# Graph layer over half of a symmetric matrix: rows of tiles taken two at a time, their mirrored products summed in one half bank

## The chip, the cores and the metric

The kernel runs on one core of a Trainium2 chip. The time is device microseconds of one execution, lower is better. A core has engines that run beside one another, each with its own queue taken in order: TensorE (PE in the profile, PEld for its weight loads), VectorE (DVE), ScalarE (ACT), GpSimd (POOL), and SyncE (SP), which here only issues transfers. SBUF is the working memory of 128 partitions; [...] DRAM is the outer memory.

## The reference

Four graph layers act in turn on x (4096 nodes, 64 features) with one symmetric, sparse 4096 x 4096 matrix adj, each followed by a residual and a layernorm: a Chebyshev layer, an attention layer with two gated units, a layer of decayed ranks, and a hyperbolic layer. The change lies in the last one, and this is what it computes:

```python
def _L3_gnn_ref(x, adj, weight, bias):
    ...
    deg = jnp.maximum(adj.sum(axis=1, keepdims=True), 1e-08)
    w = adj / deg
    log_ij = _logmap(x[:, None, :], x[None, :, :], c)
    agg = jnp.einsum('ij,ijc->ic', w, log_ij)
    transformed = agg @ weight + bias
    origin = jnp.zeros_like(transformed)
    return _expmap(origin, transformed, c)
...
x = _layernorm(x + _L3_gnn_ref(x, adj, L3_gnn_weight, L3_gnn_bias), axis=-1)
```

For every pair of nodes i, j a scalar factor f of x_i and x_j multiplies adj_ij, and the weighted rows are summed over j. Both f and adj are symmetric in i and j up to factors of one node alone, so a tile of the product serves its own rows and, turned, the mirrored ones.

## The kernel before

The 4096 nodes are eight groups of 512 (GW), each of four blocks of 128. A tile (i, j) pairs row group i with column group j, 512 x 512. `seq` is the order in which the layer before finishes the groups, and "place" is a group's index in it; below, groups are called by their place. Only tiles with the column's place not below the row's are taken: 36, row by row: (0,0), (0,1) ... (0,7), (1,1), (1,2) and so on to (7,7). Eight are diagonal, 28 are not. An off-diagonal tile is loaded twice from DRAM, once as it is (`load_own`, L1301) and once mirrored (`load_mirrored`, L1307), 1 MB each, three buffers for each kind.

The loop runs over half tiles: turn n works on half n % 2 of tile n // 2. Of a diagonal tile's second half only the right 256 columns are computed (`columns`). The steps of one half:

- `product` (L1327, PE) puts a 128 x 1024 pair of products into PSUM as v, from `rights[i]`, a pair of factors of the row (rv, ro) that `right` builds once for each row, with two matmuls and two ACT copies (L1283 to L1287). Two buffers of each are in turn.
- `square` (L1336, ACT), `less_one` (L1353, DVE), `opposite` (L1345, PE), Ln (L1520) and Exp (L1521) on ACT, rt = max(v) + rt (L1545, DVE), Exp (L1547) and Ln (L1556) on ACT, the factor f (L1530, DVE), then own = own * f (L1533, DVE), two turns later.
- `turn` transposes f on PE (L1371; L1364 for a diagonal tile) into a "post" bank of two, and DVE multiplies the mirrored tile by it (L1373, 128 x 512, four for each off-diagonal tile; L1366 for a diagonal one).
- `gather` multiplies by nat_c on PE. A row i has one PSUM bank, `sums[i]`, from a pool of two. The own product (L1387) gathers in the upper 64 partitions, over the whole row of tiles. The mirrored product of the tile before (L1392) goes to the lower 64 partitions of the same bank, starts anew with each tile, and is at the end of the tile copied (row 0, L1401) or added (L1403) by DVE to `tb`, 64 x 512, at the columns of j.
- When a row ends, ACT copies the upper half to `tb` (L1406), and `finals` puts six steps (one empty, `first` to `fifth`) into the list `seam`; one step is taken at the end of a turn. They bring the group through small matmuls, the exponential map, the layernorm (L241 to L261) and to the output. The first entries of `seam` are the last groups of the layer before (L1077 to L1120).

The Python order is not the machine order: the framework schedules each engine's queue itself, except where `in_order` fixes it; dependencies through tiles and buffers become semaphores. POOL clears the buffers of `right` (L1265) and a part of tb (L1295) at the start of the layer.

Of the kernel before, what the change touches and what calls it, by code (L numbers as in the profile page):

```python
# [9 lines left out]
F32 = mybir.dt.float32  # L10
BF16 = mybir.dt.bfloat16
# [3 lines left out]
ALU = mybir.AluOpType  # L15
# [45 lines left out]
def gnn4_kernel(  # L61
# [21 lines left out]
    nc = tc.nc  # L83
    P = 128
    N, F = x.shape
    NB = N // P
    GB = 4
    GW = GB * P
    NG = NB // GB
    CB = 4  # L90
# [56 lines left out]
    with tc.tile_pool(name="tri", bufs=1) as tri_p:  # L147
# [6 lines left out]
        lower, upper = slice(0, HP), slice(HP, P)  # L154
# [301 lines left out]
    with tc.tile_pool(name="acc", bufs=1) as acc_p, tc.tile_pool(name="win", bufs=1) as win_p, tc.tile_pool(  # L456
        name="cols0", bufs=4
    ) as cols_p, tc.tile_pool(name="diag0", bufs=2) as diag_p, tc.tile_pool(
        name="ps_t0", bufs=3, space=PSUM
    ) as ps_t, tc.tile_pool(name="ps_a0", bufs=1, space=PSUM) as ps_a, tc.tile_pool(  # L460
        name="ps_p0", bufs=2, space=PSUM
# [112 lines left out]
        for g in range(NG):  # L574
# [3 lines left out]
            for c in reversed(range(NCH)):  # L578
# [40 lines left out]
                n = g * NCH + c  # L619
# [71 lines left out]
        due, n = [], 0  # L691
# [358 lines left out]
    for signed in (True, False):  # L1050
        with tc.If(any_negative > 0) if signed else cmp.Else() as block:
            cmp = block
            with tc.tile_pool(name="cols1", bufs=4 if not signed else 2) as cols_p, tc.tile_pool(name="sign1", bufs=1 if signed else 5) as sg, tc.tile_pool(
                name="tail1", bufs=1
            ) as tl, tc.tile_pool(name="ps_a1", bufs=1 if signed else 2, space=PSUM) as ps_a, tc.tile_pool(
                name="ps_p1", bufs=2, space=PSUM
# [80 lines left out]
    with tc.tile_pool(name="mask2", bufs=3) as mk_p, tc.tile_pool(name="wt2", bufs=3) as wt_p, tc.tile_pool(  # L1137
        name="ps_c2", bufs=1, space=PSUM
# [104 lines left out]
    with tc.tile_pool(name="o3", bufs=1) as op, tc.tile_pool(name="cols3", bufs=3) as cols_p, tc.tile_pool(  # L1243
# [15 lines left out]
        wh_x = op.tile([P, F], F32, name="wh_x")  # L1259
        kappa = op.tile([P, 2, NB], F32, name="kappa")  # L1260

        rvs = [op.tile([P, GW], F32, name=f"rv{q}") for q in range(2)]
        ros = [op.tile([P, GW], BF16, name=f"ro{q}") for q in range(2)]
        for t in rvs + ros:
            nc.gpsimd.memset(t, 0.0)  # L1265

# [11 lines left out]
        nc.vector.tensor_copy(spread[:, F : F + 1], pair[:, F - 1 : F])  # L1278

        def right(i):  # L1280
            q = seq.index(i) % 2
            ps = ps_p.tile([P, GW], F32, name="post", tag="post")
            nc.tensor.matmul(ps[0 : F + 2, :], lhsT=to_right, rhs=tr_a[:, gcols(i)], start=True, stop=True)  # L1283
            nc.scalar.copy(rvs[q][0 : F + 2, :], ps[0 : F + 2, :])
            ps = ps_p.tile([P, GW], F32, name="post", tag="post")
            nc.tensor.matmul(ps[0:2, :], lhsT=to_other, rhs=tr_o[:, gcols(i)], start=True, stop=True)
            nc.scalar.copy(ros[q][0:2, :], ps[0:2, :])  # L1287
            return rvs[q], ros[q]


        seq = turns_of[0] + turns_of[1]
        tiles = [(i, j) for n, i in enumerate(seq) for j in seq[n:]]
        NT = len(tiles)
        own, mirrored = {}, {}
        nc.gpsimd.memset(tb[F:P, gcols(seq[0])], 0.0)  # L1295
# [20 lines left out]
        NU = 2 * NT  # L1316
# [59 lines left out]
        def gather(t, h, tm):  # L1376

            if t is not None:
                i, j = tiles[t]
                if i == j and h == 0:  # L1380
                    sums[i] = ps_a.tile([P, GW], F32, name="sums_ps")
                bank = sums[i]
            else:
                bank = sums[seq[-1]]
            for k in (HB * h, HB * h + 1):
                if t is not None:
                    in_order(nc.tensor.matmul(  # L1387
                        bank[0:F, :], lhsT=nat_c[:, j * CB + k, :], rhs=own[t][:, k, :],
                        start=(i == j and k == 0), stop=(j == seq[-1] and k == CB - 1), skip_group_check=True,
                    ))  # L1390
                if tm is not None:
                    in_order(nc.tensor.matmul(  # L1392
                        bank[F:P, :], lhsT=nat_c[:, tiles[tm][0] * GB + k, :], rhs=mirrored[tm][:, k, :],
                        start=(k == 0), stop=(k == CB - 1), skip_group_check=True,
                    ))
            work = []
            if tm is not None and h:
                i, j = tiles[tm]
                to = tb[F:P, gcols(j)]
                if i == seq[0]:  # L1400
                    work.append(lambda: nc.vector.tensor_copy(to, bank[F:P, :]))  # L1401
                else:
                    work.append(lambda: nc.vector.tensor_tensor(to, bank[F:P, :], to, ALU.add))  # L1403
            if t is not None and h and tiles[t][1] == seq[-1]:
                g = tiles[t][0]
                work.append(lambda: nc.scalar.copy(tb[0:F, gcols(g)], bank[0:F, :]))  # L1406
                seam.extend(finals(g))
            return work
# [99 lines left out]
        while n < NU + 2 or turns or gathers:  # L1508
            if n % 2:
                load_own((n + 1) // 2)  # L1510
                load_mirrored((n - 1) // 2)
            after = gather(*gathers.pop(n)) if n in gathers else []
            turned = [w for what in turns.pop(n, []) for w in turn(what)]
            if n < NU:
                if n % 2 == 0:
                    fs[n // 2] = fp.tile([P, CB, GW], F32, name="f3")
                w, cs = ws[n][:, :, columns(n)], columns(n)
                rts[n] = el.tile([P, HB, GW], F32, name="rt3")
                rt = rts[n][:, :, cs]
                nc.scalar.activation(w, w, AF.Ln, scale=2.0**-LN_SHIFT)  # L1520
                nc.scalar.activation(rt, w, AF.Exp, bias=half_shift[:, 0:1], scale=0.5)  # L1521
                square(n + 1)
                opposite(n + 1)
            if n >= 2 and n - 2 < NU:
                m = n - 2
                t, h = divmod(m, 2)
                cm = columns(m)
                hs = slice(h * HB, (h + 1) * HB)
                f, at = fs[t][:, hs, cm], own[t][:, hs, cm]
                nc.vector.scalar_tensor_tensor(  # L1530
                    f, rts.pop(m)[:, :, cm], T_MAX, ws.pop(m)[:, :, cm], ALU.min, ALU.mult
                )
                nc.vector.tensor_tensor(at, at, f, ALU.mult)  # L1533
                diagonal = tiles[t][0] == tiles[t][1]
                before = t - 1 if t and tiles[t - 1][0] != tiles[t - 1][1] else None
                gathers[n + 1] = (t, h, before)
                if diagonal and h == 0:
                    late_turns[n + 1] = (t, 0)
                if not diagonal and h == 1:
                    turns.setdefault(n + 1, []).append((t, 0))  # L1540
                    turns.setdefault(n + 2, []).append((t, 1))
            for work in turned:
                work()
            if n < NU:
                nc.vector.scalar_tensor_tensor(rt, vs[n][:, :, cs], V_FLOOR, rt, ALU.max, ALU.add)  # L1545
                product(n + 2)
                nc.scalar.activation(w, w, AF.Exp, bias=half_shift[:, 1:2], scale=-0.5)  # L1547
            late = turn(late_turns.pop(n)) if n in late_turns else []
            for work in after:
                work()  # L1550
            less_one(n + 1)
            for work in late:
                work()
            if 0 < n <= NU:
                rt = rts[n - 1][:, :, columns(n - 1)]
                nc.scalar.activation(rt, rt, AF.Ln, bias=one_col)  # L1556
            if seam:
                seam.pop(0)(ps_p)
            if n + 6 < NU and tiles[(n + 6) // 2][0] not in rights:
                i = tiles[(n + 6) // 2][0]  # L1560
                rights[i] = right(i)
            n += 1
        for work in seam:
            work(ps_p)
# [45 lines left out]
```

## Time and profile before

| what | value |
|---|---|
| time, median of 3 runs | 1551.27 us (1541.69, 1551.27, 1553.98) |
| the profiled execution, its own time | 1546.41 us |
| its span, first to last instruction | 1544.3 us |
| mean granted TensorE clock | 0.977 |
| busy over the span: PE, DVE, ACT, POOL | 1410.2, 1066.9, 761.4, 123.8 us |
| last layer, first work on POOL | 1067.6 us |
| first product of the last layer (L1327) | 1074.2 us |
| last add to tb (L1403) | 1522.2 us |

The profile is of one execution. A row of it names line, engine, operation, tile written <- tiles read, and shape; in groups of instructions a count and the mean duration follow. The stage table gives, for each stretch of the span, the busy time of PE, PEld, DVE, ACT and POOL in this order, then the granted clock, the share of the DMA engines and GB/s. The list of waits reads: engine and line that waited <- engine and line that released it, total us, times, the longest. [...]

### The profile page before, as it was taken

What the parts mean: (1) busy time and instruction counts of PE and PEld (TensorE: products, weight loads), DVE (VectorE), ACT (ScalarE), POOL (GpSimd) and SP (SyncE); (2) the same over time, 40 slices, a digit from 0 to 9 for tenths busy, and PEclk for the clock granted to TensorE, in tenths of its full rate; (3) what the DMA queues carried; (4) which work ended last, traced back from release to release, by engine and by line L of the source; (5) the groups of instructions that cost most, each with busy time, mean ns of one, the idle gap of its engine ahead of it and who ended that gap; (6) DMA issues with size and microseconds to landing.
All of it is one profiled execution on the core that took longest, in us unless ns stands there. A gap on an engine that the chain in (4) does not pass through costs nothing.

```text
span 1544.3 us, 19446 instructions
## 1 busy us (share of the span) xinstructions
PE 1410.2 (91%) x7054; PEld 644.7 (42%) x7054; DVE 1066.9 (69%) x2123; ACT 761.4 (49%) x1265; POOL 123.8 (8%) x194
## 2 busy tenths in 40 slices
PE   5999999999999969889899999998888999899995
PEld 4555655554443323334343333333334444344343
DVE  5899989883000663667666422556999999999997
ACT  3544434441000110222222476654877999899995
POOL 3011000000000001222222200000000000000000
PEclk9999999999999998999999999999999999999997
DMA  9999999996787987888888655553224453445430
GB/s 295 412 404 411 411 410 397 382 358 242 245 287 261 389 342 271 280 309 305 296 309 296 207 177 183 164 165 131 88 109 164 162 195 136 167 156 193 149 113 11
DMA packets 103359, 385.38 MB, mean 250 GB/s; under 512 B 16340, under 2 KB 17368, under 8 KB 71256
## 3 DMA queue, kind: packets, MB, share of 16 engines
q1 hardware_dynamic: 84256, 296.78, 53.9%
q0 software_dynamic: 15616, 85.73, 13.6%
q10 hardware_dynamic: 3384, 1.56, 0.4%
q8 instruction: 57, 0.93, 0.2%
q14 instruction: 46, 0.38, 0.1%
HBM read 297.26 MB, written 85.20 MB: 248 GB/s over the span
## 4 chain that ended last, share of the span: by engine, by line
PE 32%; DVE 18%; ACT 6%; issue 2%; DMA 2%; SPq 0%; ACTq 0%; DVEq 0%
PE v_ps L1327 5%; PE a_ps L997 4%; PE sums_ps L1387 4%; PE cnt_ps L1192 4%; PE acc_ps L1150 4%; DVE rt L1545 3%; DVE at_m L1373 3%; PE p_ps L980 2%; DVE f L1530 2%; DVE at_d L1533 2%; ACT wt L1197 2%; PE post L779 1%; DMA at<-adj_t 1%; PE p_ps L988 1%; DVE w L1353 1%
## 5 line engine op out<-in xcount | busy, mean ns | idle before, releaser
L592 ACT COPY at<-tp 128x512 f32<-128x512 f32 x256 | 132.5, 598 | 137.2 <-issue 96.0
L1327 PE MATMUL v_ps<-rv,tr_a 128*128 128x512 f32 (+1 forms) x288 | 141.5, 616 | 31.7 <-DVE rt L1545 30.3
L1197 ACT ACTIVATE wt<-cnt_ps 128x512 uint16<-128x512 f32 x208 | 115.4, 594 | 72.1 <-PE cnt_ps L1192 70.3
L585 PE MATMUL tp<-ident,raw 128*128 128x128 f32 x1024 | 133.4, 284 | 16.2 <-DMA raw<-in_adj_dram 12.0
L618 DVE TENSOR_REDUCE dpart<-raw 128x4 f32<-128x2048 f32 x64 | 145.4, 2272 | 0.4 <-DMA raw<-in_adj_dram 0.3
L620 DVE TENSOR_REDUCE lows<-raw 128x1 f32<-128x2048 f32 x64 | 145.4, 2271 | 0.0
L1387 PE MATMUL sums_ps<-at_d,nat_c 128*64 128x512 f32 x288 | 139.8, 606 | 1.4 <-DVE at_d L1533 1.0
L585 PEld LDWEIGHTS tp<-ident,raw 128*128 128x128 f32 x1024 | 116.6, 145 | 55.3 <-issue 34.1
L997 PE MATMUL a_ps<-at,nat_a 128*64 128x512 f32 x512 | 126.9, 624 | 2.9 <-DVE at L963 2.9
L447 DVE TENSOR_SCALAR pos<-at 128x2048 fp8e4<-128x2048 f32 x72 | 87.1, 1224 | 58.1 <-DMA at<-adj_t 49.3
L1392 PE MATMUL sums_ps<-at_m,nat_c 128*64 128x512 f32 x224 | 108.6, 607 | 0.0
L492 PE MATMUL w_ps<-at,cheb_n 128*128 128x512 f32 x224 | 101.1, 595 | 0.0
L492 PE MATMUL pass<-at,cheb_n 128*128 128x512 f32 x224 | 99.9, 604 | 0.7 <-DVE cheb_n L643 0.7
L1556 ACT ACTIVATE rt<-rt,one_col 128x1024 f32<-128x1024 f32 x72 | 78.7, 1095 | 22.5 <-DVE rt L1545 22.0
L1327 PEld LDWEIGHTS v_ps<-rv,tr_a 128*128 128x128 f32 x288 | 52.8, 199 | 82.7 <-DVE rt L1545 39.5
L1545 DVE SCALAR_TENSOR_TENSOR rt<-v_ps,rt 128x1024 f32<-128x1024 f32 x72 | 83.2, 1156 | 3.8 <-ACT rt L1521 3.6
L1192 PE MATMUL cnt_ps<-m,follow 128*64 128x512 fp8e4 x480 | 81.1, 391 | 4.7 <-ACT wt L1197 2.3
L1533 DVE TENSOR_TENSOR at_d<-at_d,f 128x1024 f32<-128x1024 f32 x72 | 83.2, 1156 | 0.1
L1530 DVE SCALAR_TENSOR_TENSOR f<-rt,w 128x1024 f32<-128x1024 f32 x72 | 82.9, 1158 | 0.5 <-ACT rt L1556 0.4
L1373 DVE TENSOR_TENSOR at_m<-post,at_m 128x512 f32<-128x512 f32 x112 | 75.3, 683 | 9.3 <-PE post L1371 8.6
L1336 ACT ACTIVATE w<-v_ps,one_col 128x1024 f32<-128x1024 f32 x72 | 75.7, 1053 | 11.3 <-PE v_ps L1327 10.9
L1547 ACT ACTIVATE w<-w,half_shift 128x1024 f32<-128x1024 f32 x72 | 78.7, 1094 | 0.9
(365 smaller groups left out, 2267.3 us busy)
## 6 DMA issues: line engine op xcount, KB each, us to landing
at<-adj_t SPq DMA_DIRECT2D x122, 1024.0 KB, 6.1
raw<-in_adj_dram SPq DMA_DIRECT2D x64, 1024.0 KB, 13.7
adj_t<-at POOLq DMA_DIRECT2D x64, 1024.0 KB, 8.2
at_d<-adj_t SPq DMA_DIRECT2D x36, 1024.0 KB, 4.8
at_m<-adj_t SPq DMA_DIRECT2D x28, 1024.0 KB, 6.8
mask_t<-pos POOLq DMA_DIRECT2D x64, 256.0 KB, 5.9
m<-mask_t SPq DMA_DIRECT2D x120, 128.0 KB, 2.8
m<-mask_t SPq DMA_DIRECT2D x60, 256.0 KB, 3.9
```

Of the source, the lines that this page charges most:

```text
L492: in_order(nc.tensor.matmul(ps, lhsT=cheb_n[:, jb, k : k + 2, :], rhs=rhs, start=first, stop=last))
L585: in_order(nc.tensor.transpose(tp[:, cols(b)], raw[:, b, cols(k)], ident))
L592: nc.scalar.copy(at[:, k, :], tp)
L618: in_order(nc.vector.tensor_reduce(dpart[:, g, c, :], raw, AX.X, ALU.add))
L620: in_order(nc.vector.tensor_reduce(lows[:, n : n + 1], raw.rearrange("p b j -> p (b j)"), AX.X, ALU.min))
L997: in_order(nc.tensor.matmul(ps[q * F : (q + 1) * F, :], lhsT=nat_a[:, c * CB + k, 0:F], rhs=parts[q if signed else 0][:, k, :], start=(c = ...
L1192: in_order(nc.tensor.matmul(cnt[a][r * HP : (r + 1) * HP, :], lhsT=follow, rhs=chunks[c][odd][2 * a + r][:, k, :], start=(h == 2 * NB - 1) ...
L1197: in_order(nc.scalar.activation(wt[odd][a], cnt[a], AF.Relu, scale=-128.0))
L1327: nc.tensor.matmul(vs[n][:, k, cs], lhsT=tr_a[:, cols(jb)], rhs=rights[i][0][:, cs], start=True, stop=True)
L1373: work.append(lambda to=to, tp=tp: nc.vector.tensor_tensor(to, tp, to, ALU.mult))
L1387: in_order(nc.tensor.matmul(bank[0:F, :], lhsT=nat_c[:, j * CB + k, :], rhs=own[t][:, k, :], start=(i == j and k == 0), stop=(j == seq[-1] ...
L1545: nc.vector.scalar_tensor_tensor(rt, vs[n][:, :, cs], V_FLOOR, rt, ALU.max, ALU.add)
```

## The change

`tiles` is built by pairs of rows (places 0 and 1, 2 and 3, 4 and 5, 6 and 7). The pair's own three tiles come first, (0,0), (0,1), (1,1), and then, for each later column, the tile of the first row and that of the second: (0,2), (1,2), (0,3), (1,3) and so on. The mirrored products always go to the lower half of the bank of the pair's second row, `lower`. Within the pair a mirrored tile stands alone; for a later column the two mirrored tiles are summed in that half bank, and copied or added to `tb` once, after the second. The own products stay each in its row's bank; both banks of the pool are so in use over a pair.

With this come four buffers of each factor of `right` instead of two, and a lookup that builds the factor of any row up to six turns ahead, at most one a turn; and two steps of `seam` a turn, instead of one, after turn 20 while more than seven wait.

```diff
-        rvs = [op.tile([P, GW], F32, name=f"rv{q}") for q in range(2)]
-        ros = [op.tile([P, GW], BF16, name=f"ro{q}") for q in range(2)]
+        rvs = [op.tile([P, GW], F32, name=f"rv{q}") for q in range(4)]
+        ros = [op.tile([P, GW], BF16, name=f"ro{q}") for q in range(4)]
...
-            q = seq.index(i) % 2
+            q = seq.index(i) % 4
...
-        tiles = [(i, j) for n, i in enumerate(seq) for j in seq[n:]]
+        tiles = []
+        for n in range(0, NG, 2):
+            one, two = seq[n : n + 2]
+            tiles += [(one, one), (one, two), (two, two)]
+            tiles += [(i, j) for j in seq[n + 2 :] for i in (one, two)]
+
+        def place(g):
+            return seq.index(g)
...
-            else:
-                bank = sums[seq[-1]]
+            if tm is not None:
+                i, j = tiles[tm]
+
+                lower = sums[seq[place(i) // 2 * 2 + 1]]
+                alone = place(i) // 2 == place(j) // 2
+                begins, ends = alone or place(i) % 2 == 0, alone or place(i) % 2 == 1
...
-                        bank[F:P, :], lhsT=nat_c[:, tiles[tm][0] * GB + k, :], rhs=mirrored[tm][:, k, :],
-                        start=(k == 0), stop=(k == CB - 1), skip_group_check=True,
+                        lower[F:P, :], lhsT=nat_c[:, i * GB + k, :], rhs=mirrored[tm][:, k, :],
+                        start=(begins and k == 0), stop=(ends and k == CB - 1), skip_group_check=True,
...
-            if tm is not None and h:
-                i, j = tiles[tm]
+            if tm is not None and h and ends:
                 to = tb[F:P, gcols(j)]
-                if i == seq[0]:
-                    work.append(lambda: nc.vector.tensor_copy(to, bank[F:P, :]))
+                if place(i) < 2:
+                    work.append(lambda: nc.vector.tensor_copy(to, lower[F:P, :]))
                 else:
-                    work.append(lambda: nc.vector.tensor_tensor(to, bank[F:P, :], to, ALU.add))
+                    work.append(lambda: nc.vector.tensor_tensor(to, lower[F:P, :], to, ALU.add))
...
-            if seam:
-                seam.pop(0)(ps_p)
-            if n + 6 < NU and tiles[(n + 6) // 2][0] not in rights:
-                i = tiles[(n + 6) // 2][0]
-                rights[i] = right(i)
+            for _ in range(2 if len(seam) > 7 and n > 20 else 1):
+                if seam:
+                    seam.pop(0)(ps_p)
+            for i, _ in tiles[: (n + 6) // 2 + 1]:
+                if i not in rights:
+                    rights[i] = right(i)
+                    break
```

More of the change, by code (lines that the diff above doesn't have):

```diff
@@ L1387, in gather @@
                     in_order(nc.tensor.matmul(
-                        bank[0:F, :], lhsT=nat_c[:, j * CB + k, :], rhs=own[t][:, k, :],
-                        start=(i == j and k == 0), stop=(j == seq[-1] and k == CB - 1), skip_group_check=True,
+                        bank[0:F, :], lhsT=nat_c[:, tiles[t][1] * CB + k, :], rhs=own[t][:, k, :],
+                        start=(tiles[t][0] == tiles[t][1] and k == 0),
+                        stop=(tiles[t][1] == seq[-1] and k == CB - 1), skip_group_check=True,
                     ))
```

## The prediction

> **What bounds the kernel now.** I read the page's slices first, for the stretch that the change touches, then the busy times by stage, then the waits, then the instructions in order of time on VectorE (DVE).
>
> ```profile
> PE   5999999999999969889899999998888999899995
> DVE  5899989883000663667666422556999999999997
> ACT  3544434441000110222222476654877999899995
> ```
>
> A slice is 1544.3/40 = 38.6 us. The last layer begins at about 1068 us (slice 27, counted from 0) and fills the rest. From slice 28 DVE is at 9 throughout, ScalarE (ACT) and TensorE (PE) dip to 8. By stage (busy us, instructions in brackets):
>
> ```profile
> 1100.00:1200.00 100.00, 88.80 (x361) 38.23 (x362) 94.17 (x173) 80.34 (x84) 0.00 (x0) 0.97 0.37 136
> 1200.00:1300.00 100.00, 93.10 (x393) 41.33 (x389) 97.97 (x145) 94.85 (x125) 0.00 (x0) 1.00 0.45 171
> 1300.00:1400.00 100.00, 91.14 (x369) 38.32 (x368) 91.78 (x151) 90.12 (x119) 0.00 (x0) 0.98 0.41 150
> 1400.00:1500.00 100.00, 92.23 (x385) 41.42 (x385) 93.61 (x162) 92.67 (x134) 0.00 (x0) 1.00 0.43 159
> ```
>
> The third busy column is DVE, the fourth ACT; the DMA share is under half. DVE is the longest in every row, but ACT is one to three points behind from 1200 on. The waits from 1081 to 1523 us:
>
> ```profile
> PE v_ps L1327 <- DVE rt L1545: 30.3, 33, 3.8
> ACT rt L1556 <- DVE rt L1545: 22.0, 25, 2.5
> ACT w L1336 <- PE v_ps L1327: 10.0, 7, 2.7
> DVE at_m L1373 <- PE post L1371: 8.6, 11, 2.2
> ACT w L1520 <- DVE w L1353: 6.6, 13, 1.5
> DVE rt L1545 <- ACT rt L1521: 3.6, 5, 1.5
> DVE tb L1403 <- PE sums_ps L1392: 2.2, 4, 1.0
> ```
>
> PE and ACT wait for DVE far longer than DVE for them. So an instruction off DVE's queue is worth its place there. That place is seen in DVE's own order of time:
>
> ```profile
> 1261.14 1.22 DVE L1545 SCALAR_TENSOR_TENSOR rt<-v_ps,rt 128x1024 f32<-128x1024 f32 x1
> 1262.27 0.68 DVE L1353 TENSOR_SCALAR w<-w 128x1024 f32<-128x1024 f32 x1
> ...
> 1266.34 1.22 DVE L1545 SCALAR_TENSOR_TENSOR rt<-v_ps,rt 128x1024 f32<-128x1024 f32 x1
> 1267.59 0.69 DVE L1403 TENSOR_TENSOR tb<-sums_ps,tb 64x512 f32<-64x512 f32 x1
> 1268.31 0.43 DVE L1353 TENSOR_SCALAR w<-w 128x512 f32<-128x512 f32 x1
> ```
>
> Without an add, w (L1353) starts 1.13 us after rt; with it, 1.97 us after (1268.31 - 1266.34). One add costs **0.84 us** of DVE, though its own row is 0.69.
>
> [...]
>
> **The change, part by part.**
>
> *Removed.* 28 mirrored tiles, each with one DVE copy or add today (7 on L1401, 21 on L1403). After it, the four tiles inside a pair (0,1), (2,3), (4,5), (6,7) keep theirs, and each later column of a pair has one for both rows: 6 + 4 + 2 = 12. That is 16, and the order of the built programs shows 7 copies and 9 adds. Twelve fewer: 6 in rows 0 and 1, 4 in rows 2 and 3, 2 in rows 4 and 5. At 0.84 us: 10.1 us of DVE. Weighted with DVE's share where they lie (0.96 over 1100 to 1300, 0.92 over 1300 to 1400, 0.94 over 1400 to 1500): 0.84 x (6 x 0.96 + 4 x 0.92 + 2 x 0.94) = **9.5 us**. What is late next? From start to start in 1250 to 1256, ACT takes some 5.1 us for its five functions of half a tile, 10.2 a tile. DVE takes 2 x (3 x 1.13 + 0.60) + 4 x 0.60 + 0.84 = 11.2, and with half an add 10.8. DVE stays the longer by 0.6, so the cut is not eaten by ACT between rows. Where the finals run, ACT and DVE are even (92.67 and 93.61), and the two adds there may bring nothing: 0 to 1.7 us less. I take 1 off.
>
> *PE.* Same matmuls, weights and start flags in number; summing costs nothing more. The wait of a product for the add before it (L1387 for L1403, 0.3 us in all) comes half as often: nothing. New is that in 12 tiles (6 + 4 + 2: the own product of a pair's first row beside the mirrored one of its second) the two halves go to two banks. The nearest row is L1162 of the layer before, whose 64-column products go to four banks in turn: four start within 0.01 us of 1065.18 and four more at about 1065.43, each lasting 0.38: two banks at once are no hindrance there. So 0; the other end is rival D.
>
> *Moved.* Tiles, with their transfers (36 of 1 MB on L1301, 28 on L1307, all on SP's queue, same count and same lead of three half tiles). Landing takes 4.8 and 6.8 us at a DMA share of 0.41; three half tiles are about 17 us. Covered: 0. The eight right factors (2 matmuls, 2 ACT copies of 0.58 and 0.57 us each) stay eight; the second row's moves to the first turn, where ACT sat idle 7.79 us before L1284; it borrows a post buffer there: 0 to +1. Four more buffers mean four more POOL memsets (0.5 us each, 1067.64 on) ahead of ro's and tb's: ro's first would be filled at about 1070.1, its copy comes at 1074.05; tb's next reader comes at 1202. Hidden, 0.
>
> *Finals.* Two rows finish two half tiles apart, so twelve steps queue where six did; the loop takes two a turn while more than seven wait. Same DVE and ACT work, in lumps, beside two light diagonal tiles: 0 to +3, I take +0.5. Both banks of a pair fall free before the next pair opens them: the copy of each half comes three half tiles ahead. The end: eleven steps are left after the loop before, ten after, and the last add to the end takes 1544.3 - 1522.2 = 22 us in a chain of small steps. Group 5's layernorm (some 2.5 us on DVE) falls just after the last add instead of just before, where DVE is busy 11.31 of 21.3 us: 0 to +1, taken +0.
>
> *Sum.* -9.5 + 1 + 0.5 = **-8 us**. The profiled execution took 1546.41 (span 1544.3), so 1538.4; against the median shown, 1551.27, it would be 1543.3. The profiled one lies 4.9 below that median and inside the 12.3 us spread of the three; I go between, from a base of 1549: **1541**.
>
> **Rivals.**
> A, the forecast: DVE sheds twelve adds and stays the bound. For it: 92 to 98% busy, and w directly behind each add. 1541. Chance 0.70.
> B, more than the adds: w stands behind the add, ACT's Ln waits for w (6.6 us) and the next rt for ACT, so queue and stalls go together. DVE idles about 22.5 us in 1100 to 1500; a third of it back makes -16: 1533. Against: DVE's longest waits are for transposes (8.6), which the change keeps. 0.13.
> C, hidden: ACT, so close behind, or the lumped finals take the place of DVE. -3 to +1 about the base: 1548. Against: ACT idles for DVE 28.6 us, DVE for ACT 4.4. 0.11.
> D, slower: halves in two banks do not run side by side. A pair of products takes 0.43 us (1253.89 to 1254.32); in turn, 0.43 more, eight pairs a tile, 3.5 us on PE in twelve tiles, 41 us. PE is free some 9% of an 11.5 us tile, 1 us; so 2.5 x 12 = 30 come through, less 8: +22, 1571. It decides from 1.7 us a tile (12 x (1.7 - 1) = the gain). Against: L1162. 0.06.
> That the change does not do what it says is excluded by the order of the programs.
>
> **Numbers.** About 1% (15.5 us) is what a measurement of this kernel can tell from no change. Faster by over that (under 1535.8): B and a sliver of A, 0.16. Slower: D, 0.06. Within: 0.78. The range takes A on either base, most of B, and C: 1531 to 1553.
>
> **What would show it.** Right: the tb rows on DVE are 7 and 9; the stretch from the first tile to the last add shortens by about 8; the end stays 22 us; L1353 follows L1545 at 1.13 us in tiles that lost an add. Wrong for A: DVE's idle time grows by the 9 us it sheds (C), or the mirrored products no longer start 0.01 us after the own ones in the twelve tiles (D), or DVE's waits for transposes shrink (B).

## The result, and the profile after

The changed kernel takes **1566.58 us** (median of six, 1562.22 to 1568.44) against 1547.77 (median of six, 1541.69 to 1553.98) for the one before: ratio 1.0113, 95% interval 1.0090 to 1.0136. It is slower, by 17.5 us from the ratio and by 18.8 from the medians, where 8 less were forecast. The profiled execution has a span of 1566.7 us (before: 1544.3).

The adds went as forecast. The groups of instructions on tb, DVE alone (after the count: minimum, median and maximum in ns, first and last start in us):

```profile
L1416 DVE TENSOR_TENSOR tb<-sums_ps,tb x9: 694/694/696, 1320.2 to 1545.1; 64x512 f32<-64x512 f32 x9
L1414 DVE COPY tb<-sums_ps x7: 694/695/696, 1131.4 to 1292.9; 64x512 f32<-64x512 f32 x7
```

Seven copies and nine adds; from the last add to the end 1566.7 - 1545.1 = 21.6 us, where 22.1 were before. DVE is busy 1061.3 us in all, 5.6 less. Yet the slices of the page and the stages have holes:

```profile
PE   5999999999999869889899999997979998999894
...
DVE  5889988982002664656677223647899989888886
ACT  3544443431000111212222575645879888988984
```

```profile
1100.00:1200.00 100.00, 88.23 (x349) 37.56 (x350) 93.23 (x172) 83.64 (x86) 0.00 (x0) 0.97 0.35 130
1200.00:1300.00 100.00, 93.76 (x391) 40.59 (x388) 91.19 (x128) 87.67 (x106) 0.00 (x0) 1.00 0.46 175
1300.00:1400.00 100.00, 89.91 (x350) 37.29 (x350) 88.22 (x132) 90.77 (x113) 0.00 (x0) 0.98 0.40 150
1400.00:1500.00 100.00, 88.27 (x349) 38.87 (x346) 85.90 (x151) 85.22 (x128) 0.00 (x0) 0.96 0.41 150
```

DVE fell from 97.97 to 91.19 in the second row and from 93.61 to 85.90 in the last, and ACT fell with it (94.85 to 87.67, and 92.67 to 85.22). PE rose by 0.66 in the second row and fell by 3.96 in the last, where all three are idle more. That is the picture of engines waiting for one another in turn. The waits from 1081 us to the last add, 1545 us:

```profile
PE v_ps L1336 <- DVE rt L1558: 28.5, 32, 3.6
ACT rt L1569 <- DVE rt L1558: 27.5, 21, 2.8
...
DVE at_m L1382 <- PE post L1380: 19.4, 16, 4.9
ACT w L1345 <- PE v_ps L1336: 19.4, 20, 1.8
...
DVE rt L1558 <- ACT rt L1534: 9.1, 7, 2.7
...
ACT v L1472 <- PE post L1468: 8.2, 6, 3.6
DVE w L1362 <- ACT w L1345: 5.8, 8, 1.8
```

The first row hardly changed (30.3 before). New is the other direction: DVE for transposes 19.4 (8.6), DVE for ACT's Exp 9.1 (3.6), and ACT for PE's matmuls of the finals 8.2 (1.8). ACT also waits longer for PE's products v, 19.4 (10.0).

The granted clock does not explain the loss. Its mean is 0.973, where it was 0.977; in the last row it is 0.96 against 1.00, but the kernel before took 1551.77 us in one execution with a mean of 0.969.

The longest of DVE's stalls for a transpose, first in DVE's order of time, then in PE's (columns: start, duration, instruction; idle time and its releaser in square brackets):

```profile
1366.84 1.23 DVE L1558 SCALAR_TENSOR_TENSOR rt<-v_ps,rt 128x1024 f32<-128x1024 f32 x1
1367.98 0.68 DVE L1362 TENSOR_SCALAR w<-w 128x1024 f32<-128x1024 f32 x1
1373.59 1.29 DVE L1382 TENSOR_TENSOR at_m<-post,at_m 128x512 f32<-128x512 f32 x2 [4.93 <-PE post L1380]
```

```profile
1366.86 1.02 PE L1283 MATMUL post<-tr_a,to_right 128*66 128x512 f32 x2
1367.81 0.38 PE L1286 MATMUL post<-sp_two,to_other 128*2 128x512 bf16 x1
1368.12 1.07 PE L1400 MATMUL sums_ps<-at_d,nat_c 128*64 128x512 f32 x2
1369.12 1.98 PE L1336 MATMUL v_ps<-rv,tr_a 128*128 128x512 f32 x4
1371.03 0.64 PE L1406 MATMUL sums_ps<-at_m,nat_c 128*64 128x512 f32 x1
1371.04 0.64 PE L1400 MATMUL sums_ps<-at_d,nat_c 128*64 128x512 f32 x1
...
1372.89 1.09 PE L1380 MATMUL post<-ident,f 128*128 128x128 f32 x8
```

Each of these fp32 matmuls has two records in the trace (L1400 has 288 for 144 in the program). Behind the matmuls of `right` one own product runs alone (1368.12, two records), then the two products v of a later half tile (1369.12, four records), and only then the mirrored partner of the first (1371.03). So the gather is cut in two and the transposes come late. Such cuts, places where a mirrored product does not stand directly behind an own one, number 3 in the kernel before and 10 in the one after, by PE's order in both traces. They are possible because `in_order` ties a matmul only to the tied one before it: the matmuls of `right`, of the finals and of v are not tied, and the framework has put products v into the gather.

Where nothing lies between, the two halves do go side by side. The next half tile, in PE's order of time:

```profile
1378.46 0.59 PE L1400 MATMUL sums_ps<-at_d,nat_c 128*64 128x512 f32 x1
1378.46 0.59 PE L1406 MATMUL sums_ps<-at_m,nat_c 128*64 128x512 f32 x1
1378.89 0.59 PE L1400 MATMUL sums_ps<-at_d,nat_c 128*64 128x512 f32 x1
1378.89 0.59 PE L1406 MATMUL sums_ps<-at_m,nat_c 128*64 128x512 f32 x1
```

These are own products of tile (2,6) and mirrored ones of (3,5), into the banks of places 2 and 3 (a bank is here one `sums_ps`, a tile of 128x512 fp32 in PSUM into which TensorE writes): 0.43 us a pair of records, as into one bank before:

```profile
1253.41 0.64 PE L1387 MATMUL sums_ps<-at_d,nat_c 128*64 128x512 f32 x1
1253.42 0.64 PE L1392 MATMUL sums_ps<-at_m,nat_c 128*64 128x512 f32 x1
1253.89 0.59 PE L1387 MATMUL sums_ps<-at_d,nat_c 128*64 128x512 f32 x1
1253.90 0.59 PE L1392 MATMUL sums_ps<-at_m,nat_c 128*64 128x512 f32 x1
```

### The profile page after: what moved, and what is told of

It reads as the page before. It is cut to its first block, busy times and chain, and to the rows that moved or that the text cites. A ratio compares the mean times of both kernels' runs of the same rounds, so it can differ in the third digit from the quotient of the medians.

```text
span 1566.7 us, 19451 instructions
## 1 busy us (share of the span) xinstructions
PE 1420.0 (91%) x7054; PEld 646.9 (41%) x7054; DVE 1061.3 (68%) x2111; ACT 761.6 (49%) x1265; POOL 125.9 (8%) x198
## 4 chain that ended last, share of the span: by engine, by line
PE 65%; DVE 19%; issue 5%; DMA 5%; ACT 5%; ACTq 1%; SPq 1%; POOL 0%; DVEq 0%; POOLq 0%
PE tp L585 7%; PE pass L492 6%; PE w_ps L492 6%; PE v_ps L1336 5%; PE sums_ps L1400 5%; PE a_ps L997 4%; PE cnt_ps L1192 4%; PE acc_ps L1150 4%; PE h_ps L485 3%; PE pass L485 3%; DVE rt L1558 3%; DVE at_m L1382 2%; PE p_ps L980 2%; PE post L506 2%; DMA at<-adj_t 2%
## 5 line engine op out<-in xcount | busy, mean ns | idle before, releaser
L585 PE MATMUL tp<-ident,raw 128*128 128x128 f32 x1024 | 133.7, 284 | 13.6 <-POOL none_t L192 6.2
L1400 PE MATMUL sums_ps<-at_d,nat_c 128*64 128x512 f32 x288 | 142.7, 616 | 3.6 <-DVE at_d L1375 2.1
L1406 PE MATMUL sums_ps<-at_m,nat_c 128*64 128x512 f32 x224 | 111.0, 614 | 0.0
L1558 DVE SCALAR_TENSOR_TENSOR rt<-v_ps,rt 128x1024 f32<-128x1024 f32 x72 | 83.6, 1160 | 9.4 <-ACT rt L1534 9.1
L1382 DVE TENSOR_TENSOR at_m<-post,at_m 128x512 f32<-128x512 f32 x112 | 74.6, 686 | 20.2 <-PE post L1380 19.4
L1345 ACT ACTIVATE w<-v_ps,one_col 128x1024 f32<-128x1024 f32 x72 | 76.0, 1058 | 19.6 <-PE v_ps L1336 19.4
```

Source lines behind the costliest of these rows:

```text
L585: in_order(nc.tensor.transpose(tp[:, cols(b)], raw[:, b, cols(k)], ident))
L1400: in_order(nc.tensor.matmul(bank[0:F, :], lhsT=nat_c[:, tiles[t][1] * CB + k, :], rhs=own[t][:, k, :], start=(tiles[t][0] == tiles[t][1] a ...
L1406: in_order(nc.tensor.matmul(lower[F:P, :], lhsT=nat_c[:, i * GB + k, :], rhs=mirrored[tm][:, k, :], start=(begins and k == 0), stop=(ends ...
```

## The experiments

Each kernel is compared with the one before on the same chip (medians there: 1545.64 us beside e1 to e4, 1548.44 beside e5 to e8, 1547.82 beside e9 to e12, 1546.61 beside e13 to e16, 1548.16 beside e17 and e18). Differences between two kernels are therefore taken from their ratios, times 1548 us; where the medians' own difference is told, it says so. The last five columns are from each kernel's trace: rt (L1545 before, L1558 after) runs once a turn, and the time is taken from its first start to that of turns 30, 52, 66 and 71 (the last), and then to the end of the span. At these turns both orders have done the same set of tiles. What lies ahead of the first rt is left out, since the untouched second layer makes it vary from 1077 to 1088.

Two cautions on this table. The intervals reach 0.0012 to 0.0039 to each side, 2 to 6 us, so a difference of some 4 us between two kernels is at the edge of what the ratios can tell. Each trace is one execution, and six executions of the kernel before spread over 12.3 us. And the turns have no sharp borders, since rt does not stand at the same place among DVE's work in every kernel: turns 30 and 31 take 9.5 us in after and 12.6 in e4. A single stretch is therefore good to some 3 us.

| kernel | us | ratio [95%] | 30 | 52 | 66 | 71 | last rt to end |
|---|---|---|---|---|---|---|---|
| before | 1547.77 | | 185.1 | 319.6 | 403.3 | 430.5 | 32.5 |
| after | 1566.58 | 1.0113 [1.0090, 1.0136] | 181.3 | 318.7 | 411.0 | 443.2 | 37.7 |
| e1 | 1553.79 | 1.0073 [1.0043, 1.0103] | 181.0 | 313.4 | 398.7 | 428.2 | 40.9 |
| e2 | 1565.82 | 1.0129 [1.0102, 1.0157] | 184.3 | 319.4 | 406.7 | 439.5 | 41.9 |
| e3 | 1563.26 | 1.0115 [1.0081, 1.0148] | 184.4 | 318.2 | 407.4 | 435.5 | 40.1 |
| e4 | 1552.54 | 1.0037 [1.0015, 1.0058] | 174.7 | 305.4 | 391.4 | 427.6 | 38.7 |
| e5 | 1547.06 | 0.9990 [0.9968, 1.0012] | 188.4 | 320.3 | 405.5 | 434.6 | 31.2 |
| e6 | 1549.07 | 1.0008 [0.9994, 1.0022] | 176.7 | 305.6 | 395.2 | 425.4 | 40.5 |
| e7 | 1548.77 | 1.0015 [0.9994, 1.0035] | 178.0 | 309.6 | 397.2 | 433.1 | 34.6 |
| e8 | 1557.57 | 1.0068 [1.0049, 1.0087] | 186.4 | 317.3 | 405.1 | 431.7 | 41.1 |
| e9 | 1573.58 | 1.0167 [1.0137, 1.0198] | 186.8 | 311.4 | 390.5 | 418.3 | 74.8 |
| e10 | 1558.02 | 1.0076 [1.0050, 1.0102] | 174.7 | 295.9 | 371.5 | 399.0 | 74.7 |
| e11 | 1570.30 | 1.0137 [1.0098, 1.0176] | 181.7 | 304.1 | 381.4 | 407.7 | 75.5 |
| e12 | 1551.23 | 1.0031 [1.0011, 1.0052] | 176.7 | 307.5 | 396.9 | 427.1 | 41.8 |
| e13 | 1543.91 | 0.9987 [0.9968, 1.0007] | 178.9 | 316.8 | 398.7 | 427.7 | 31.8 |
| e14 | 1550.50 | 1.0017 [1.0002, 1.0032] | 184.6 | 324.4 | 406.3 | 435.3 | 31.2 |
| e15 | 1557.68 | 1.0069 [1.0044, 1.0094] | 186.0 | 312.9 | 397.5 | 431.0 | 41.6 |
| e16 | 1553.02 | 1.0041 [1.0028, 1.0053] | 185.3 | 318.7 | 399.9 | 428.1 | 40.7 |
| e17 | 1547.85 | 0.9991 [0.9971, 1.0012] | 176.7 | 306.6 | 399.7 | 429.0 | 32.9 |
| e18 | 1553.03 | 1.0034 [1.0017, 1.0051] | 174.7 | 303.7 | 397.4 | 427.5 | 39.7 |

### Which part costs: e1 to e4

**e1**: the changed kernel with one step of the finals a turn, as before.

```diff
-            for _ in range(2 if len(seam) > 7 and n > 20 else 1):
-                if seam:
-                    seam.pop(0)(ps_p)
+            if seam:
+                seam.pop(0)(ps_p)
```

> The changed kernel with one step of the finals a turn throughout, as before the change. Three theories of the 19 us. S (split pairs): in PE's queue of the changed kernel ten gathers have other products between the own and the mirrored ones, three before; each costs DVE some 2 us of waiting for transposes. This kernel has five: S expects half of the loss back, about 1556 to 1559. L (lumps): two rows' finals at once, two steps a turn, starve the tiles: L expects most of it back, less a longer end, 1548 to 1552. B (the sum itself: two banks, or a wait at the half bank): 1565 to 1568, no change.

By the ratios 6 us less than after, by the medians 12.8, by the traces from the first rt (480.9 and 469.1) 11.8; and still 11 over before by the ratio. This lies between what S and L expected. The rule of two steps costs, and isn't the whole. In the trace 5 of the 10 cuts are left, though nothing was tied.

**e2**: the changed kernel with 28 copies and adds again, pairs and the rest kept.

```diff
-                begins, ends = alone or place(i) % 2 == 0, alone or place(i) % 2 == 1
+                begins, ends = True, True
...
-                if place(i) < 2:
+                if place(i) == 0:
```

> The changed kernel with each mirrored tile added alone again (28 copies and adds in place of 16), tile order, finals and the bank of the mirrored product as changed. B expects the loss to go, about 1550. S counts 13 split gathers and 12 adds of 0.84 us more: 1578 to 1584. L, whose lumps stay: 1566 plus the adds, 1574 to 1577.

By the ratios 2.5 us more than after, which is nothing within the intervals; none of the three theories expected that. Up to turn 30 the adds show (184.3 to 181.3); from there to the end they do not, and e2 does not lose more although its trace has 13 cuts. So the sum was not what slowed the kernel (B is out); its gain was eaten.

**e3**: the kernel before with its order of tiles and its adds, but the finals of an even place held until the next row ends, and the rule of two steps.

```diff
-                seam.extend(finals(g))
+                held.extend(finals(g))
+                if seq.index(g) % 2:
+                    seam.extend(held)
+                    held.clear()
...
-            if seam:
-                seam.pop(0)(ps_p)
+            for _ in range(2 if len(seam) > 7 and n > 20 else 1):
+                if seam:
+                    seam.pop(0)(ps_p)
```

> The kernel before (rows one by one, 28 adds) with the finals of rows 0, 2, 4, 6 held back until the next row ends, so that two rows' finals come at once, and with the rule of two steps a turn. L expects most of the loss without the change: 1560 to 1566. S counts three split gathers, as in the kernel before: 1545 to 1552. The end should stay as it is (rows 6 and 7 end two tiles apart in both).

As slow as after, 17.8 us over before, without any pair of rows: holding the finals, so that two groups' finals come at once (a lump), together with the rule is enough. But it does not get there by cuts. Its trace has 3, as before, and DVE's idle time from turn 30 to 66 is 13.6 us, where before has 13.3. Of the 12.6 us that this trace has over before's from the first rt on, some 6 lie between turns 30 and 71, and 7.6 after the last rt, where no change was expected.

**e4**: the changed kernel with the matmuls of `right`, `first` and `second` tied into Python's order too.

```diff
-            nc.tensor.matmul(ps[0 : F + 2, :], lhsT=to_right, ...)
+            in_order(nc.tensor.matmul(ps[0 : F + 2, :], lhsT=to_right, ...))
```

(and so L1286, L1456, L1467, L1468)

> The changed kernel with PE's products of the finals and of the right factors kept in program order, so that the scheduler cannot put later products between own and mirrored ones: two split gathers are left of ten. Work and lumps unchanged. S expects eight times some 2 us back: 1548 to 1553. L and B expect no change, 1563 to 1569, or more, as pinned work can wait where it stood free.

12 us less than after (14.0 by the medians, 14.6 by the traces), with 2 cuts instead of 10. DVE's waits for the transposes in e4 (idle time, times):

```profile
its engine sat idle before it (us, times) until:
  PE post L1380: 13.2, 20
```

They were 19.4 in 16, and 8.6 in 11 before. From turn 30 to 66, DVE's idle stretches over 0.15 us sum to 13.3 us before, 27.9 after, 15.1 in e4 and 15.6 in e1; the stretch itself takes 218.3, 229.7, 216.7 and 217.7. Taken from turn 32 to 68 instead, the stretch is 218.5 before, 231.4 after, 217.6 in e4 and 218.2 in e1. So e1 and e4, by different means, both remove most of the stalls there.

### Taken together: e5 to e8

**e5**: the ties of e4 in the kernel before.

> Control: the kernel before with PE's products of the finals and right factors kept in program order, as in e4; one split gather of three is left. If pinning is worth something of its own, this gains some 2 us a split, 1540 to 1543; if it only mends what the lumps break, 1544 to 1548, no change.

No change: one of the row order's 3 cuts is left, so the two that went had cost nothing that can be seen, and kernels with ties may be held against e5.

**e6**: e1 and e4 together.

> The changed kernel with one step of the finals a turn and the pinned order together. If lumps and splits are two separate costs, their gains of 12.8 and 14 us add up and the twelve adds show: 1538 to 1543. If they are one cost seen twice, 1550 to 1554, as each alone. The end (from the first half of tile (6,6)) should stay some 10 us longer than in the kernel before in both cases, if it is the finals of rows 4 and 5 that lengthen it.

Together 16 us less than after, by the traces 15.0, where e1 and e4 singly have 11.8 and 14.6 there: by the traces, largely two cures of one ill. The ratios do not decide this: 6 and 12 singly against 16 together could also be two separate gains. The time is that of before, and against e5 the row of the table tells why it is no better: at turn 52 e6 is 14.7 us ahead (10.4 at turn 54), at turn 71 9.2, at the end 0.1 behind. The stretch after the last rt has 9.3 us more.

**e7**: e6, but pairs for rows 0 to 3 only; rows 4 to 7 come in rows.

```diff
+            if n >= PAIRED:
+                tiles += [(i, j) for i in (one, two) for j in seq[seq.index(i) :]]
+                continue
```

(with PAIRED = 4, and `lower` the row's own bank from there on)

> e6 with rows 4 to 7 taken one by one as in the kernel before, only rows 0 to 3 in pairs: ten of the twelve adds go, and the finals of row 4 come out three tiles before those of row 5. If the late finals of rows 4 and 5 cost the end its 10 us, that comes back: 1534 to 1540, faster than the kernel before. If the end is long for another reason, or the pairs themselves cost, 1546 to 1552.

The time is e6's, and not 1534 to 1540, as it would be if the end's 10 us came back. The end is better by 5.9 us, but turn 66 to 71 now takes 35.9 us, where e5 takes 29.1: the loss moved ahead of the last rt.

**e8**: e3 without its rule of two steps.

> e3 (rows one by one, the finals of two rows released together) without the rule of two steps a turn. If two steps a turn are what costs, 1546 to 1550; if it is that two rows' finals come late and together, above all at the end, 1558 to 1566, as e3.

The rule costs 7 us here (1.0115 to 1.0068); holding the finals alone costs 10.5 against before (its trace has 5 cuts, two more than e3's, so the rule's price here isn't one of cuts), and the stretch after the last rt grows from 32.5 to 41.1.

### Without finals beside the tiles: e9 to e12

In **e9** (e5), **e10** (e6) and **e11** (e10 with the 28 copies and adds of e2) all finals come after the last tile; nothing is left out.

```diff
-                seam.extend(finals(g))
+                held.extend(finals(g))
...
-        for work in seam:
+        for work in seam + held:
```

> The kernel before, pinned as in e5, with the finals of all eight groups taken after the last tile. It is the base for the next two: the loop of tiles runs without finals, which all come in the end, so the time says little by itself (some 30 to 60 us more). What counts is the stretch from the first to the last rt on DVE: 434.6 us in e5, less some 6 us of DVE for each of the six groups whose finals lay in it, 395 to 405.

> e6 (pairs, twelve adds fewer, pinned) with all finals after the last tile, to be set against e9: the tiles without any finals beside them. If the twelve adds are worth 0.84 us each as forecast and only the finals hid it, the stretch from first to last rt is 10 us shorter than in e9, and so is the time. If an add is worth 0.5 us (rows 0 and 1 of the changed kernel against e2), 6 us. If the order by pairs itself costs, 0 or less.

> e10 with each mirrored tile added alone, 28 copies and adds in place of 16: the price of twelve adds by itself. 10 us more than e10 if an add is worth 0.84 us, 6 if 0.5, none if ACT or PE bounds the tiles.

Here the adds can be weighed alone. e11 - e10 is 9.4 us by the ratios, 12.3 by the medians and 407.7 - 399.0 = 8.7 in the tiles, so 0.7 to 1.0 us for each of the twelve. Pair order with the saved adds is worth 14 us by the ratios (e9 - e10) and 19.3 in the tiles (418.3 - 399.0), more than the 10 expected. The order by itself does not cost: e11, with all 28 copies and adds in pair order, is 4.6 us under e9 by the ratios and 10.6 in the tiles. And the finals: to have them beside the tiles saves 1.0167 - 0.9990, 27 us, in row order (e9, e5), but 1.0076 - 1.0008, 10.5 us, in pair order (e10, e6). These 17 us are what eats the 14. The four intervals together leave some 7 us of doubt on each side of the 17. e9 missed its own expectation: its tiles are 16 us shorter than e5's, where 30 to 40 were expected, so in row order much of the finals had been hidden already.

**e12**: e6 with an empty step behind each step of places 0 and 1, to thin out the first lump.

```diff
-                seam.extend(finals(g))
+                for step in finals(g):
+                    seam.extend([step, nothing] if place(g) < 2 else [step])
```

> e6 with an empty step after each step of the finals of rows 0 and 1, so that their twelve steps spread over 24 turns instead of 12. If finals in successive turns are what costs in the middle (tiles (2,2) to (3,4)), 3 to 5 us less than e6: 1543 to 1546. If only their amount counts, 1547 to 1550, as e6.

3.6 us slower than e6, where 3 to 5 less or no change were expected: no stretch of the table gets shorter by more than 0.2.

### Where the lump falls: e13 to e18

**e14**, **e15** and **e16** are e5 with one lump: the finals of one place wait for the next row's, places 0, 2 and 4 in turn.

```diff
-                seam.extend(finals(g))
+                held.extend(finals(g))
+                if seq.index(g) != 0:
+                    seam.extend(held)
+                    held.clear()
```

(2 and 4 in the others). **e13** is e7 with PAIRED = 2: rows 0 and 1 as a pair, so that two groups' finals come together where e14's do, and six adds fewer.

> The changed kernel with its matmuls of right and finals in Python's order and one step a turn, and only rows 0 and 1 taken as a pair, rows 2 to 7 in rows as before: 22 adds, six fewer than before. Theory END (what the pair order loses is that a second group's finals fall into the last tiles): from row 2 on all is as before, the loss is gone and six adds are left, 6 x 0.84 = 5 us: some 1543, ratio 0.997. Theory LUMP (twelve steps together cost wherever they fall, about 3 us for each pair of rows): 5 - 3 = 2 us, some 1546, 0.9985. Theory ORDER (pairs hide finals worse even here): 1550 or more.

> The kernel before with those matmuls in order, one change: the finals of place 0 wait until row 1 ends, and come with those of place 1; 28 adds, nothing left out. END: nothing, 1547 +/- 2, ratio 0.999. LUMP: a third of the nine us of the three lumps held together, 1550, 1.001.

> The same with the finals of place 2 held until row 3 ends. END: little, 1547 to 1550. LUMP: 1550, 1.001.

> The same with the finals of place 4 held until row 5 ends, three tiles before the end. END: nearly all of the nine us, 1554 to 1557, ratio 1.004 to 1.007, and most of it after turn 66. LUMP: 1550, 1.001.

The stretch after the last rt, by engine (the columns of the stage table), first e14, then e16:

```profile
1520.40:1551.70 31.30, 13.04 (x80) 8.17 (x79) 22.48 (x96) 14.21 (x66) 0.00 (x0) 0.78 0.06 13
```

```profile
1512.90:1553.50 40.60, 18.30 (x106) 13.50 (x104) 27.86 (x125) 18.81 (x88) 0.00 (x0) 0.70 0.06 14
```

and before, then after:

```profile
1511.80:1544.30 32.50, 14.77 (x80) 9.84 (x78) 22.16 (x96) 13.96 (x66) 0.00 (x0) 0.71 0.05 13
```

```profile
1529.00:1566.70 37.70, 18.13 (x100) 11.40 (x98) 25.90 (x116) 16.53 (x75) 0.00 (x0) 0.73 0.06 15
```

An early lump leaves the end as it was (96 DVE instructions). It costs 4 us by the ratios (e14 - e5), but their intervals overlap and the traces differ by 0.8 from the first rt on, so this price isn't established; a late one leaves 125 DVE instructions for after the last rt, and 9.5 us more there. The middle one (e15) does so too, 118 instructions and 41.6 us, though its rows end 14 half tiles earlier: one step a turn doesn't clear twelve before the next group's come. It costs most, 12 us, more than either theory allowed; e16 costs 8, as END expected, since up to turn 71 it is 6.5 us ahead of e5, the finals that it has put off. So END's cause is borne out, in e15 even where END did not expect it: a lump whose backlog reaches the last tile adds 9.5 to 10.4 us after it. LUMP's some 3 us for a lump that is cleared in time are neither shown nor excluded.

e13 against e14 is the cleanest trial of the adds beside finals: 4.6 us by the ratios (some 4 to each side), 6.6 by the medians, for six of them with the paired two rows, and at turns 30, 52, 66 and 71 it is ahead by 5.7, 7.6, 7.6 and 7.6. It is the fastest kernel of the study, 0.9987 [0.9968, 1.0007] of before: not a difference that these runs establish.

**e17** and **e18** are e7 and e6 without the finals' empty first step for places 2 to 5: a shorter list, the same work.

```diff
-            return [nothing, first, second, third, fourth, fifth]
+            steps = [first, second, third, fourth, fifth]
+            return steps if 2 <= place(g) < 6 else [nothing] + steps
```

> e7 (matmuls in order, one step a turn, rows 0 to 3 in pairs) with the empty first step of the finals left out for places 2 to 5, so that the list is shorter by one entry a group and the computation is the same. Counted from the code, 13 steps of finals are left after the last half tile's turn, where e7 has 16 and the order of before 14. Theory END (the steps left set the stretch after the last rt): that stretch falls from 34.6 to 31 or 32 us, and the time by about 3 to 1545, or below by what e7 lost in the last three tiles. If the steps left are not the cause (two groups' finals cost by coming together): 34 us stay, 1548 to 1550.

> e6 (all rows in pairs, matmuls in order, one step a turn) with the same empty steps left out: 16 steps left after the last half tile's turn instead of 18. END: the stretch after the last rt falls from 40.5 to 35 to 38 us, the time by some 4 to 1545. Otherwise: 40 us and 1549.

e17's profile bears the count out in part: 34.6 falls to 32.9, and turn 66 to 71 from 35.9 to 29.3; the time is 4 us under e7's by the ratios, 0.9 by the medians, and by its interval not distinct from before's. e18 is a miss: 40.5 falls to 39.7, not to 38, and the time is 4 above e6's. Counted from the code for every order, 13 or 14 steps left after turn 71 went with 31.2 to 32.9 us (before, e5, e13, e14, e17), 16 with 34.6 to 41.9 (after, e2, e4, e7, e18), 17 to 20 with 40.1 to 41.8 (e1, e3, e6, e8, e12, e15, e16). The count gives the direction, not the size. Part of the miss is in the count itself, which takes in the empty steps: without them e17 has 11 left where e7 has 14, but e18 has 14 where e6 has 15.

## Why the prediction was wrong

**Removed** held as a price, where nothing stood in its way. Twelve adds were put at 9.5 us and brought 9.4 (e10, e11); six were put at 5 and brought 4.6 (e13, e14). That these agree to some tenths is luck: the same differences are 8.7 to 12.3 and 4.6 to 7.6 by the other measures. In the changed kernel itself the adds brought 2.5 us or nothing (e2), so the part of the term that took 1 off for what other waits eat was too small. The chain of two instructions (w 1.13 us behind rt, at 1374.80 and 1375.93) is as forecast.

**PE** held, and rival D is out: see the pairs at 0.43 us. The mirrored products take 614 ns a record in the mean (L1406) where they took 607 (L1392), the own ones, which sum as before, 616 where they took 606: no cost of the added sum shows. **Moved** was right in the transfers: none of the waits listed for the last layer is for one. Beside the memsets, taken as hidden at 0, one DVE instruction takes 1.64 us instead of 0.35 (see the last section), but no cost for the kernel is seen. From the first matmul of the layer before's last groups (L1114) to the first copy of rv (L1284) it is 4.4 us in after and 3.8 before, but the eight kernels that clear four buffers range from 2.9 to 5.3 there, and the twelve that clear eight from 3.1 to 4.6. The factors of the later rows weren't only their 0 to +1 of work: their matmuls are among the places where the gather is cut (1366.86 above).

**The step that failed is "Finals"**: "in lumps, beside two light diagonal tiles: 0 to +3, I take +0.5". It counted the work of DVE and ACT, which is indeed the same, and neither the order on PE nor how much of that work stays hidden when it comes in lumps. The finals and `right` put matmuls outside the fixed order at the end of turns; the gather behind them is cut, its transposes come late, DVE stalls up to 4.93 us, and rt, on which the next half tile's ACT and PE work hangs, comes late with it. From turn 30 to 66 the kernel took 11.4 us more than before, though four adds had gone, and DVE's idle time rose by 14.6; in e4, with the ties, both are back near before's. The two-a-turn rule, which the step named and priced within the same 0 to +3, is worth 6 to 13 us by itself (e1), the ties 12 to 14.6 (e4), both together 15 to 17.5 (e6; ratios, traces, medians). What is left when both are mended is the other half: finals beside the tiles save 17 us less in pair order than in row order (e5, e6, e9, e10). So the term taken at +0.5 measured some 17 us (the end, next, is part of them), and the missing ties and the rule some 16 more. Rival C came nearest ("the lumped finals take the place of DVE"), at -3 to +1: it saw the gain eaten, not a loss of 17.5 us, and named neither cuts nor the end.

**"The end" failed too**: "eleven steps are left after the loop before, ten after ... taken +0". That count is right, but was made at the wrong place. The loop goes on for three turns after the last half tile's; after turn 71 the list and the groups still to come make 14 steps before, 16 after, and 18 where one is taken a turn. Only the part after the last add was priced (22 us, now 21.6), while the time grew ahead of it: from turn 66 to 71 by 5.0 us and from the last rt to the end by 5.2. In e6, where the stalls are mended, this is what remains: 9.3 us more than in e5 after the last rt, about as much as the adds bring.

The sum of the trace from the first rt: turn 0 to 30 -3.8, 30 to 66 +11.4, 66 to 71 +5.0, after it +5.2, together +17.9 but for rounding (463.0 to 480.9). Of what the prediction named as signs, the one for C showed: DVE's idle time grew by more than it shed.

Three things stay open. That the cuts as such, and not the changed order on PE at large, cost what e4 won back is likely from the stall shown, but not shown apart: in e5 two cuts went for nothing, and e2 has 13 and is no slower than after. e3 reaches after's time with 3 cuts, so there the finals cost in another way, which its trace only places (after turn 30, and more than half of it after the last rt). And e18, with one step of work fewer at the end, came out above e6, by 4 us from the ratios and 1.3 from the traces.

## What to carry to other kernels

When an order of loops is changed, follow the small work that runs in its shadow: when it becomes ready, how many steps are still open when the last large piece is done (count there, not at the end of the loop), and what it puts between the large instructions on the engine that isn't the bound. A saved instruction of the bounding engine was not worth its price in every kernel here: twelve adds brought 9.4 us with no finals beside the tiles (e10, e11), and in the changed kernel 2.5 us, which is nothing within the intervals (e2); moving all shadow work behind the loop, in both orders, is a cheap way to weigh the two apart. And where a scheduler orders a queue, side work that isn't tied to the order can cut a fixed sequence in two, here in 10 places, and in 2 with the ties (e4).

## What the runs showed of the hardware

**A DVE instruction beside POOL's memsets.** At the start of the layer, in after, by DVE's and by POOL's order of time:

```profile
1073.80 1.64 DVE L1268 TENSOR_SCALAR to_right<-ident 64x64 f32<-64x64 f32 x1
```

```profile
1073.48 1.92 POOL L1265 MEMSET ro<- 128x512 bf16 x4
1075.45 0.52 POOL L1304 MEMSET tb<- 64x512 f32 x1
```

and in the kernel before:

```profile
1069.61 0.52 POOL L1295 MEMSET tb<- 64x512 f32 x1
...
1069.83 0.35 DVE L1268 TENSOR_SCALAR to_right<-ident 64x64 f32<-64x64 f32 x1
```

The same small instruction takes 1.64 us instead of 0.35, and ends at 1075.44, when POOL's four memsets in a row have ended (1073.48 + 1.92 = 1075.40). In the traces of all kernels it has 1.640 to 1.647 us where eight buffers are cleared (twelve kernels, after among them), and 0.348 to 0.352 where four are (eight). Before, too, it ends just behind a memset (1069.61 + 0.52 = 1070.13, against 1070.18), so 0.35 need not be its time when alone. So its longer time goes with the eight memsets in every trace; what makes it longer, no run here tells, and that the kernel's time suffered is not shown.

**All engines less busy.** From 1400 to 1500 us DVE, ACT and PE fell together, by 7.71, 7.45 and 3.96 us of 100. No work was added to any of them; less of it gets done in such a stretch. Read one engine at a time, each looks as if it had room, and only the waits between them show what is wrong (from 1081 us to the last add, DVE's for transposes 19.4 us, 8.6 before).
